# A Fourier neural operator on one core: the next image's beginning dealt out four pieces sooner, its statistics behind the row copies, ten head steps in a new order

## The chip, the cores and the metric

One core of a Trainium2 chip runs the whole program. The metric is device time in microseconds (us) for one execution of all eight images; lower is better. Five engines work side by side[...]: TensorE (PE in the profile, with its weight loads as PEld), VectorE (DVE), ScalarE (ACT), GpSimd (POOL) and SyncE (SP, which here only starts transfers).

## What is computed

For each of 8 images (8 channels of 256x256, four groups of two channels) the reference normalizes x by group, runs a Fourier neural operator and adds x; then it normalizes the sum by group, takes a 3x3 maximum around each pixel, and adds again.

```python
h = _gconv1x1(concat(x, grid), fc0_w, fc0_b)
for i in range(4):                       # the four "layers"
    h1 = _spectral_conv(h, sp_w1[i], sp_w2[i])   # rfft2, 24x12 modes kept and mixed, irfft2
    h2 = _gconv1x1(h, w_w[i], w_b[i])
    h = h1 + h2
    if i < 3:
        h = _gswish(h, betas[i])
h = _gswish(_gconv1x1(h, fc1_w, fc1_b), betas[3])   # 10 -> 128 per group
return _gconv1x1(h, fc2_w, fc2_b)                   # 128 -> 2 per group: "the head"
x = x + that;  x = x + dilate3x3(_gn(x))
```

## The kernel before, in words

Everything is float32. An image's state h lies in SBUF as 11 chunks of rows (`NCH`), each 128 partitions x 4 x 512. A layer has three parts. `mix` (line 403) multiplies the kept modes by the layer's weights on VectorE: twelve operations n = 0 to 11, products (L411) and sums (L414) in turn. `rows_even` (L474) or `rows_odd` (L496) turns the mixed spectrum into values for every row: TensorE writes p_g in PSUM, and VectorE (L217) and ScalarE (L215) copy it to the tile zt. `layer` (L534) then runs a `burst` per chunk (L580): TensorE adds the 1x1 convolution (L590, or L587 in layer 0) and the inverse transform along the row (L593, reads zt) into p_z, and ScalarE writes p_z back to h (L598, or L600 in layer 3). In layer 3 each chunk of h is then stored to DRAM.

Two further streams are woven into the layers.

- The head of the image before: 128 steps f (`first`, L803: TensorE L813, then ScalarE L814 and L815 into a tile act, of which there are 4) and 64 steps c (`second`, L818: TensorE L830 on two act tiles, then a VectorE addition L839, or L837 for the first of an output tile). The addition of a step c follows at once; that of a step C is only put into VectorE's queue at the next f (`sum_up`, L772).
- The next image's beginning, `start` (L673): `spectrum_x` (L265, statistics of x, its normalization and its small spectrum) and then `mix` for layer 0. It is a Python generator; each `yield` in it ends a piece, and whoever holds the generator takes a piece with `next`.

No scheduler decides the order: the block under `tc.manual_schedule` (L919) takes PE, DVE, ACT and SP instructions as the generators give them out. Each string that `layers` yields is a list of head steps to be put in at that place (`step`, L899); "t" takes a piece of the dilation of the image before that (`tail`).

In layer 3, the generator of the next image is taken from at 24 places: once after each of the two halves of `rows_odd` (L523), and twice per chunk in `layer`: after the steps "fct", and again after the "f" behind them (L612 and L615). Here "side piece" means such a piece, "first place" and "second place" mean those two. What is left of the generator after layer 3 is taken in `rest` (L680), one piece at a time, each followed by the steps of one entry of `REST` (L43); after each entry one chunk of the next image's x (two for image 0) is read into h (`read_x`, four transfers on SP).

PSUM has two rings: "one", two buffers of a bank, and "tri", two of three banks. A burst, a step f, the p_g of a half of the rows, and the fold p_f (L455) take one of each (`ps_four`); a step c and each TensorE piece of `spectrum_x` take a "one" (`ps_a`). A buffer comes free when the copy that reads it is done.

While image 0 runs there is no head, and only image 0's own pieces fill the queues; the code calls this `alone`.

Of the kernel before, what the change touches and what calls it, by code (L numbers as in the profile page):

```python
# [34 lines left out]
NCH = 11  # L35
# [4 lines left out]
DR = 2  # L40
STEPS = 128
BEHIND = mybir.DependencyInfo(mybir.DependencyClass.Sync, mybir.DependencyReason.DATA)
REST = ("ff", "f", "f", "fC", "fc"), ("f", "fc", "ffC", "ff", "fc")  # L43


@with_exitstack
def fno_dilate_kernel(ctx: ExitStack, tc: tile.TileContext, a: dict, out: bass.AP):
# [11 lines left out]
    def ps_a(name):  # L59
        return ps.tile([128, 512], F32, tag="one", bufs=2, name=name)  # L60
# [8 lines left out]
    def part(i):  # L69
        return slice(32 * i, 32 * i + 32)  # L70


    n_img = a["x"].shape[0]
# [191 lines left out]
    def spectrum_x(b, out_):  # L265

        x = turned[:, 0:2].rearrange("p i (g f) -> p i g f", g=G)
        st = sb.tile([128, G, 2, 6], F32, tag="bn", bufs=1, name=f"bn_x{b}")
        for i in range(2):
            for g in range(G):  # L270
                nc.vector.bn_stats(st[:, g, i, :], x[:, i, g])
            yield
        mv = sb.tile([128, G, 2], F32, tag="mvx", name=f"mv_x{b}")
        for g in range(G):
            nc.vector.bn_aggr(mv[:, g], st[:, g].rearrange("p n s -> p (n s)"))
        yield
        yield
        yield
        p = ps_a(f"p_st_x{b}")
        group_means(p, mv[:, :, 0])  # L280
        mr = sb.tile([128, 2, G + 1], F32, tag="mrx", name=f"mr_x{b}")
        d = sb.tile([128, 2, G + 1], F32, tag="dx", bufs=1, name=f"d_x{b}")
        nc.vector.tensor_copy(mr[:, 0], p[:, : G + 1])
        dm = d[:, 0, :G]
        nc.vector.tensor_tensor(dm, mv[:, :, 0], mr[:, 0, :G], ALU.subtract)
        nc.vector.tensor_tensor(dm, dm, dm, ALU.mult)
        nc.vector.tensor_tensor(dm, dm, mv[:, :, 1], ALU.add)
        yield
        yield
        q = ps_a(f"p_sv_x{b}")  # L290
        group_means(q, dm)
        nc.vector.tensor_scalar(d[:, 1], q[:, : G + 1], EPS, None, ALU.add)
        rsqrt(d[:, 1], mr[:, 1], d[:, 0])
        out_["mr"] = mr[:, :, G]
        for g in range(G):
            nc.vector.tensor_scalar(
                x[:, :, g], x[:, :, g], mr[:, 0, g : g + 1], mr[:, 1, g : g + 1], ALU.subtract, ALU.mult)
            if g != 1:
                yield
        yield  # L300

        a1, a2 = turned[:, 2, 0:512], turned[:, 2, 512:1024]
        a3 = turned[:, 2, 1024:1216].rearrange("p (g m) -> p g m", g=G)
        nc.vector.memset(a3, 0.0)
        p = ps_a(f"p_a1_{b}")
        for i in range(2):
            for g in range(G):
                mm(p[part(g)], er[:, i, :], x[:, i, g], start=i == 0, stop=i == 1)
        nc.vector.tensor_copy(a1, p)
        yield  # L310
        yield
        t = ps_a(f"p_a2_{b}")
        for i in range(4):
            nc.tensor.transpose(t[:, 128 * i : 128 * (i + 1)], a1[:, 128 * i : 128 * (i + 1)], ident)
        nc.vector.tensor_copy(a2, t)
        yield
        yield
        p = ps_a(f"p_a3_{b}")
        for j in range(2):
            for i in range(2):  # L320
                mm(p[:, 24 * j : 24 * j + 24], a2[:, 256 * j + 128 * i : 256 * j + 128 * i + 128], fw[:, i, 0:24],
                   start=i == 0, stop=i == 1)
        for g in range(G):
            nc.vector.tensor_copy(a3[part(g), g, :], p[part(g), 0:48])
        yield
        yield
        cols = a3.rearrange("p g (j k) -> p g j k", j=2)
        p = ps_a(f"p_xs_{b}")
        for k in range(2):
            for term in range(2):  # L330
                for q in range(4):
                    k0 = 12 * term + 3 * q
                    mm(p[part(q), 24 * k : 24 * k + 24], unf[:, spectrum_table(k, term), :],
                       cols[:, :, :, k0 : k0 + 3], start=term == 0, stop=term == 1)
        xe4 = xe.rearrange("p (s k) g j -> p s g j k", s=2)
        for k in range(2):
            nc.vector.tensor_copy(
                xe4[:, k, :, 0:2, :],
                p[:, 24 * k : 24 * k + 24].rearrange("p (g j k) -> p g j k", g=G, j=2),
            )  # L340
        yield
        bt = sb.tile([128, 2, 3, G, WID], F32, tag="B", bufs=1, name=f"B_{b}_0")
        prod = turned[:, 0, :1200].rearrange("p (i g o j) -> p i g o j", i=6, g=G, o=WID)
        for i in range(6):
            nc.vector.tensor_tensor(
                prod[:, i], wext, xe[:, i].unsqueeze(2).to_broadcast([128, G, WID, 5]), ALU.mult
            )
        nc.vector.tensor_reduce(
            bt.rearrange("p s k g o -> p (s k g o)"),
            prod.rearrange("p i g o j -> p (i g o) j"), AX.X, ALU.add,  # L350
        )
        out_["bt"] = bt
        yield
        yield

    def spectrum_table(k, term):

# [45 lines left out]
    def mix(b, l, out_):  # L403
# [3 lines left out]
        for n in range(12):  # L407
            k, k2 = n // 4, n // 2 % 2
            pr = turned[:, 2, 1024 * k2 : 1024 * k2 + 800].rearrange("p (g m i) -> p g m i", g=G, i=WID)
            if n % 2 == 0:  # L410
                nc.vector.tensor_tensor(  # L411
                    pr, sw[k], bt[:, k2, k].unsqueeze(2).to_broadcast([128, G, 2 * WID, WID]), ALU.mult)
            else:
                nc.vector.tensor_reduce(  # L414
                    s[k2][:, k].rearrange("p s o g -> p (s o) g"),
                    pr.rearrange("p g m i -> p m g i"), AX.X, ALU.add,
                )
            if l == 0:
                if n % 2 or n > 7:
                    yield  # L420
            elif n not in (0, 2, 6, 10):
                yield {1: "fc", 4: "fC", 7: "fC", 9: "fC"}.get(n, "f")
            if n == 2 and l == 3 and b + 1 < n_img:
                load_x(b + 1)
# [71 lines left out]
    def rows_odd(b, l, side):  # L496

        zv = zt[:, :, :, : NBLK * WID].rearrange("p r g (n o) -> p g o n r", n=NBLK)
        hold()
        yield "ffc"  # L500
        for part_of, by_act, kinds in ((((0, 1, 2), (3, 4, 5)), (2, 3), "fc"), (((9,), (6, 7, 8)), (1, 4, 5), "f")):
            one, tri, banks = ps_four(f"p_g_{b}_{l}_{part_of[0][0]}")
            pairs = []
            for i, os in enumerate(part_of):
                for at, o in enumerate(os):
                    for j in range(NQ):
                        for k in range(2):
                            two = slice(64 * k, 64 * k + 64)
                            last = mm(banks[2 * i + k][part(j), 2 * NBLK * CS * at : 2 * NBLK * CS * (at + 1)],
                                      fz2[two, o, :], rowg[two, j].rearrange("p g x -> p (g x)"),  # L510
                                      start=True, stop=True)
                for k in range(2):
                    src = banks[2 * i + k][:, : 2 * NBLK * CS * len(os)]
                    src = src.rearrange("p (o g n r) -> p g o n r", g=2, n=NBLK, r=CS)
                    dst = zv[:, 2 * k : 2 * k + 2, os[0] : os[-1] + 1]
                    if len(os) == 1:
                        pairs.append((dst[:, :, 0], src[:, :, 0]))
                    else:
                        pairs += [(dst[:, g], src[:, g]) for g in range(2)]
            copy_banks(pairs, by_act)  # L520
            yield kinds
            if l == 3:
                next(side, None)  # L523
        hold(last)
        if l < 3:
            yield "t"


    def read_x(b, c):
        if b < n_img:  # L530
            for g in range(G):
                nc.sync.dma_start(h[32 * g : 32 * g + 6, c].rearrange("p f w -> p (f w)"), a["xp"][b, c, g])
# [146 lines left out]

    def rest(b, then):  # L680
        c = 0 if b == 0 else NCH - 4
        for n, _ in enumerate(then):
            yield REST[b > 0][n]
            for _ in range(2 if b == 0 else 1):
                if c < NCH:
                    read_x(b + 1, c)
                    c += 1
        for i in range(c, NCH):
            read_x(b + 1, i)

    def layers(b, stored, d, then, ahead):

# [431 lines left out]
```

## Time and profile before

| what | value |
|---|---|
| median of 3 runs (lowest to highest) | 3705.54 us (3701.52 to 3706.05) |
| the profiled execution: time, and the span of its instructions | 3705.41 us, 3703.6 us |
| PE, DVE, ACT busy (share of the span) | 3495.7 us (94%), 2385.4 us (64%), 2864.6 us (77%) |
| mean granted TensorE clock | 0.977 |
| layer 3's rows of images 1, 2, 5, 6, from the first p_g to the first L593 of burst 0 | 9.9 us each; 10.8 us in images 3 and 4 |
| the last burst of layer 3 (first L593) to the fold p_f of the next image | 20.0 us in images 1, 2, 4, 5; 21.7 us in images 3 and 6 |

The page's first section gives each engine's busy time; its fourth the chain of work that ended last, by engine and line; its fifth the groups of equal instructions, with the idle time of the engine just before them and what ended it. A line of the timeline gives start, duration, engine, source line, operation, "out<-in", shapes, and in brackets the idle time ahead and who ended it. A line of the waits gives who waited for whom, the total in us, how often, and the longest.

### The profile page before, as it was taken

What the parts mean: (1) busy time and instruction counts of PE and PEld (TensorE: products, weight loads), DVE (VectorE), ACT (ScalarE), POOL (GpSimd) and SP (SyncE); (2) the same over time, 40 slices, a digit from 0 to 9 for tenths busy, and PEclk for the clock granted to TensorE, in tenths of its full rate; (3) what the DMA queues carried; (4) which work ended last, traced back from release to release, by engine and by line L of the source; (5) the groups of instructions that cost most, each with busy time, mean ns of one, the idle gap of its engine ahead of it and who ended that gap; (6) DMA issues with size and microseconds to landing.
All of it is one profiled execution on the core that took longest, in us unless ns stands there. A gap on an engine that the chain in (4) does not pass through costs nothing.

```text
span 3703.6 us, 112658 instructions
## 1 busy us (share of the span) xinstructions
PE 3495.7 (94%) x50872; PEld 1271.0 (34%) x50872; DVE 2385.4 (64%) x3711; ACT 2864.6 (77%) x3021; POOL 117.1 (3%) x202
## 2 busy tenths in 40 slices
PE   5768999999999999999999999999999999999997
PEld 2323333333333333333333333333333333333222
DVE  6776666557775677746776577765777567772443
ACT  2435888888788888787887878888888878879986
POOL 1000000000000000000000000000000000000000
PEclk7878999999999999999999999999999999999998
DMA  3005111432225212261223512244222522225221
GB/s 91 16 19 205 52 50 46 160 110 72 72 83 190 81 55 66 92 220 52 60 62 125 181 55 74 65 159 122 64 75 89 183 76 61 72 64 194 82 83 48
DMA packets 114081, 344.71 MB, mean 93 GB/s; under 512 B 15985, under 2 KB 18481, under 8 KB 98177
## 3 DMA queue, kind: packets, MB, share of 16 engines
q1 hardware_dynamic: 95392, 276.32, 24.6%
q0 software_dynamic: 18208, 61.18, 5.0%
q8 instruction: 400, 6.55, 0.7%
q14 instruction: 81, 0.66, 0.1%
HBM read 213.44 MB, written 123.74 MB: 91 GB/s over the span
## 4 chain that ended last, share of the span: by engine, by line
PE 73%; DVE 16%; issue 4%; ACT 4%; DMA 2%; POOL 0%; ACTq 0%; DVEq 0%; POOLq 0%
PE p_fc L830 20%; PE p_fc L813 19%; PE p_z L593 9%; PE p_z L590 7%; PE p_d L558 7%; PE p_z L587 3%; DVE y L839 3%; PE p_u L572 3%; DVE turned L541 3%; DVE S L414 3%; DVE turned L411 2%; DMA yin<-y_rows 2%; PE p_b L381 1%; ACT act L815 1%; ACT act L814 1%
## 5 line engine op out<-in xcount | busy, mean ns | idle before, releaser
L815 ACT ACTIVATE act<-p_fc 128x1536 f32<-128x1536 f32 x1024 | 1493.1, 1458 | 0.0
L813 PE MATMUL p_fc<-hs,c_w 32*128 32x512 f32 x8192 | 1133.2, 625 | 40.2 <-DVE y L839 20.8
L830 PE MATMUL p_fc<-act,c_w 128*32 128x512 f32 x8192 | 1008.6, 601 | 0.2 <-ACT act L815 0.2
L814 ACT ACTIVATE act<-p_fc 128x512 f32<-128x512 f32 x1024 | 616.5, 602 | 229.7 <-PE p_fc L813 218.2
L541 DVE STREAM_TRANSPOSE turned<-h 128x1024 f32<-128x1024 f32 x528 | 632.7, 1226 | 189.7 <-ACT h L598 189.2
L598 ACT ACTIVATE h<-p_z 128x512 f32<-128x512 f32 (+1 forms) x528 | 511.9, 1021 | 212.2 <-PE p_z L593 212.2
L839 DVE TENSOR_TENSOR y<-p_fc,y 128x512 f32<-128x512 f32 x392 | 267.7, 683 | 553.9 <-PE p_fc L830 553.9
L813 PEld LDWEIGHTS p_fc<-hs,c_w 32*128 32x128 f32 x8192 | 357.7, 183 | 612.8 <-ACT act L814 253.3
L830 PEld LDWEIGHTS p_fc<-act,c_w 128*32 128x32 f32 x8192 | 221.8, 109 | 705.0 <-issue 330.7
L593 PE MATMUL p_z<-c_binv,zt 32*128 32x256 f32 x5632 | 411.7, 406 | 2.1 <-DVE zt L217 2.1
L590 PE MATMUL p_z<-h,c_wt 32*32 32x512 f32 x8448 | 363.5, 606 | 15.7 <-DVE zt L217 7.7
L593 PEld LDWEIGHTS p_z<-c_binv,zt 32*128 32x128 f32 x5632 | 259.8, 187 | 312.4 <-issue 300.0
L558 PE MATMUL p_d<-turned,c_fw 32*32 32x480 f32 (+1 forms) x9216 | 307.8, 539 | 0.6 <-DVE turned L541 0.2
L600 ACT ACTIVATE h<-p_z,c_bias 128x512 f32<-128x512 f32 (+1 forms) x176 | 186.4, 1110 | 89.1 <-PE p_z L593 89.0
L562 ACT ACTIVATE turned<-p_d 128x1440 f32<-128x1440 f32 x144 | 182.9, 1270 | 89.7 <-PE p_d L558 86.5
L215 ACT ACTIVATE zt<-p_g 128x198 f32<-128x198 f32 (+2 forms) x118 | 53.4, 575 | 182.8 <-PE p_g L487 99.9
L414 DVE TENSOR_REDUCE S<-turned 128x80 f32<-128x800 f32 x192 | 189.0, 984 | 5.9
L411 DVE TENSOR_TENSOR turned<-t,B 128x800 f32<-128x800 f32 x192 | 188.7, 983 | 0.9
L558 PEld LDWEIGHTS p_d<-turned,c_fw 32*32 32x32 f32 x9216 | 127.0, 103 | 165.8 <-issue 64.9
L372 DVE STREAM_TRANSPOSE turned<-zt 128x960 f32<-128x960 f32 x96 | 176.8, 1865 | 2.5
L590 PEld LDWEIGHTS p_z<-h,c_wt 32*32 32x32 f32 x8448 | 93.2, 103 | 186.8 <-DVE y L839 48.8
L572 PE MATMUL p_u<-turned,c_stack 128*32 128x480 f32 (+1 forms) x1152 | 136.7, 543 | 11.6 <-DVE turned L561 6.2
(192 smaller groups left out, 1762.8 us busy)
## 6 DMA issues: line engine op xcount, KB each, us to landing
stored<-h SPq DMA_DIRECT2D x88, 1024.0 KB
hs<-stored SPq DMA_DIRECT2D x352, 256.0 KB
t<-in_spw SPq DMA_DIRECT2D x96, 400.0 KB
yin<-y_rows POOLq DMA_DIRECT2D x56, 512.0 KB, 5.2
h<-in_xp SPq DMA_DIRECT2D x352, 48.0 KB
turned<-in_xw SPq DMA_DIRECT2D x16, 1024.0 KB
y<-in_x SPq DMA_DIRECT2D x56, 256.0 KB
y_rows<-y POOLq DMA_DIRECT2D x56, 256.0 KB, 3.9
```

Source lines behind the costliest of these rows:

```text
L411: nc.vector.tensor_tensor(pr, sw[k], bt[:, k2, k].unsqueeze(2).to_broadcast([128, G, 2 * WID, WID]), ALU.mult)
L414: nc.vector.tensor_reduce(s[k2][:, k].rearrange("p s o g -> p (s o) g"), pr.rearrange("p g m i -> p m g i"), AX.X, ALU.add,)
L541: nc.vector.transpose(dst[:, 2 * i : 2 * i + 2], h[:, c, 2 * i : 2 * i + 2].rearrange("p f (s x) -> p f s x", s=2))
L558: mm(banks[q][part(v % 4), : 240 * n], fw8[part(q), v, :], t[part(q), :, :, v, : NBLK * WID], start=v < 4, stop=v >= 4)
L590: mm(o, wt[part(q), l, g, :], h[part(q), c, f, :], start=True, stop=False)
L593: mm(banks[q][:, HW * s : HW * (s + 1)], zt[part(q), 2 * c + s].rearrange("p f o -> p (f o)"), binv[part(q), :], start=False, stop=s == 1)
L598: nc.scalar.activation(dst, src, AF.Silu)
L813: mm(banks[g], w1[part(g), blk, :], hs[k][part(g), :], start=True, stop=True)
L814: nc.scalar.activation(act[:, 0, :], one, AF.Silu)
L815: nc.scalar.activation(act[:, 1:4, :], tri, AF.Silu)
L830: mm(acc[part(g), :], w2[:, g, 15 - rb - i : 47 - rb - i], act[:, g, :], start=i == 0, stop=i == 1)
L839: nc.vector.tensor_tensor(y, sums, y, ALU.add)
```

## The change

Three things move; no arithmetic is added or taken away.

1. In `rows_odd` of layer 3 both pieces of the next image are taken behind the second half's copies and steps, no longer one behind each half. These pieces are the statistics of x: twice four bn_stats (L271).
2. Four yields are deleted: one behind the aggregation in `spectrum_x`, one behind its end, and two in layer 0's `mix` (n = 8 and n = 10). Later pieces so come one place sooner, then two, then four. All twelve operations of `mix` now lie in layer 3, where operations 8 to 11 stood in `rest`.
3. `rest` takes the two pieces left (the sums L432 and L433, then the fold) behind an entry of ten head steps in all, split in two; the reads of x follow an entry in lots of up to six chunks. Written as one row, the steps were "f fc ffC ff fc" and are "ffc ffCffcf"; for image 0 they were "ff f f fC fc" and are "fff ffCfc".

```diff
-REST = ("ff", "f", "f", "fC", "fc"), ("f", "fc", "ffC", "ff", "fc")
+REST = ("fff", "ffCfc"), ("ffc", "ffCffcf")
...
             nc.vector.bn_aggr(mv[:, g], st[:, g].rearrange("p n s -> p (n s)"))
         yield
         yield
-        yield
         p = ps_a(f"p_st_x{b}")
...
         out_["bt"] = bt
-        yield
         yield
...
             if l == 0:
-                if n % 2 or n > 7:
+                if n % 2:
                     yield
...
             copy_banks(pairs, by_act)
             yield kinds
-            if l == 3:
-                next(side, None)
+        for _ in range(2 if l == 3 else 0):
+            next(side, None)
         hold(last)
...
         c = 0 if b == 0 else NCH - 4
-        for n, _ in enumerate(then):
+        if b + 1 == n_img:
+            return
+        for n in range(2):
             yield REST[b > 0][n]
-            for _ in range(2 if b == 0 else 1):
-                if c < NCH:
-                    read_x(b + 1, c)
-                    c += 1
-        for i in range(c, NCH):
-            read_x(b + 1, i)
+            for i in range(c + 6 * n, min(c + 6 * n + 6, NCH)):
+                read_x(b + 1, i)
+            next(then, None)
```

## The prediction

> **What bounds the kernel now.** I read the page first: TensorE is busy 94% of the span, no other engine over 77%, and the chain that ended last runs 73% on TensorE. So what counts is where TensorE stands still.
>
> ```profile
> PE 3495.7 (94%) x50872; PEld 1271.0 (34%) x50872; DVE 2385.4 (64%) x3711; ACT 2864.6 (77%) x3021; POOL 117.1 (3%) x202
> PE 73%; DVE 16%; issue 4%; ACT 4%; DMA 2%; POOL 0%; ACTq 0%; DVEq 0%; POOLq 0%
> ```
>
> The waits of TensorE have two rows at the edited places (columns: us in total, times, longest).
>
> ```profile
> PE p_fc L813 <- DVE y L839: 20.8, 41, 1.8
> PE p_z L590 <- DVE zt L217: 7.7, 6, 1.3
> ```
>
> The second comes once in each of images 1 to 6, in layer 3's rows; image 2's timeline shows it:
>
> ```profile
> 1128.28 1.20 PE L509 MATMUL p_g<-c_rowg,fz 64*32 64x132 f32 x64
> 1129.03 2.46 DVE L271 BATCH_NORM_STATS2 bn_x<-turned 128x6 f32<-128x512 f32 x4
> 1129.52 1.09 ACT L215 ACTIVATE zt<-p_g 128x132 f32<-128x132 f32 x3 [1.01 <-PE p_g L509]
> 1131.40 1.06 DVE L217 COPY zt<-p_g 128x132 f32<-128x132 f32 x3
> 1131.83 1.92 PE L590 MATMUL p_z<-h,c_wt 32*32 32x512 f32 x32 [1.27 <-DVE zt L217]
> 1133.69 1.15 PE L593 MATMUL p_z<-c_binv,zt 32*128 32x256 f32 x16
> ```
>
> p_g is ready at 1129.48, but VectorE is at x's statistics until 1131.49; burst 0 needs that PSUM back. The other stall is behind layer 3, where `mix` stands ahead of a head addition:
>
> ```profile
> 1209.75 0.99 DVE L414 TENSOR_REDUCE S<-turned 128x80 f32<-128x800 f32 x1
> 1210.65 0.68 DVE L839 TENSOR_TENSOR y<-p_fc,y 128x512 f32<-128x512 f32 x1
> 1211.39 1.14 PE L813 MATMUL p_fc<-hs,c_w 32*128 32x512 f32 x8 [1.81 <-DVE y L839]
> ```
>
> [...] just behind these stalls the clock column (the last but two) falls to half for 3.4 us at 1571.5 and 2015.3 (rows, images 3 and 4), 1653.5 and 2974.4 (behind layer 3, images 3 and 6).
>
> ```profile
> 1562.70:1571.50 8.80, 7.52 (x198) 3.48 (x194) 7.14 (x16) 7.09 (x10) 0.00 (x0) 1.00 0.18 50
> 1571.50:1574.90 3.40, 3.40 (x43) 1.53 (x46) 2.19 (x4) 0.01 (x1) 0.00 (x0) 0.50 0.12 34
> ```
>
> [...] both waits shown above are for PSUM.
>
> **The change part by part**, per image, against the profiled 3705.4 us (span 3703.6; the median of the runs, 3705.5, is the same within 0.1).
>
> *Rows: −1.97 us in each of images 1 to 6.* With the eight bn_stats behind the copies, VectorE's three copies run 1129.5 to 1130.55 (1.06), ScalarE's end at 1130.61 as before. The head step ends near 1130.5, so burst 0 starts there and its large part at 1130.67; L590 to L593 takes 1.07 elsewhere (1186.80 to 1187.88). L593 at 1131.7 instead of 1133.69. Cover: the eight (4.9 us) end at 1135.5, just as the next head addition falls due (step c ends 1135.5); were they later, burst 1 would wait for it. Image 0 has no head; there L593 waits for zt itself (2.10 us, at 300.22) and could start at 298.1; its chain of side pieces moves along: −2.0.
>
> *Four pieces sooner: +2.40 us in images 2 to 6, +0.47 in image 1.* This is the hidden cost. The built order shows each TensorE side piece going from the second place (behind f) to the first (between c and f). Its "one" buffer shifts the ring: the f behind it now waits for the addition of the c just ahead, and the burst for the side piece's copy (or, for p_a L314 and L321 of images 2 to 6, for that f's ScalarE pass). From image 2:
>
> ```profile
> 1171.28 1.14 PE L813 MATMUL p_fc<-hs,c_w 32*128 32x512 f32 x8
> 1171.38 0.69 DVE L839 TENSOR_TENSOR y<-p_fc,y 128x512 f32<-128x512 f32 x1 [4.18 <-PE p_fc L830]
> 1172.35 0.66 PE L314 MATMUL p_a<-ident,turned 128*128 128x128 f32 x4
> 1173.10 0.24 PEld L590 LDWEIGHTS p_z<-h,c_wt 32*32 32x32 f32 x32 [0.34 <-ACT act L814]
> ```
>
> Let E be the end of c (1171.28). The addition lets f go at E+0.86 (1171.38 + 0.69 + 0.05 to start), or behind the side piece if that is longer. Then burst is 1.82 later where it waits for f's ScalarE pass (1171.28 to 1173.10), else 1.08, or when the copy is done. E to burst, before and after: p_st 1.83, 2.38 (0.86 + 1.08 would be 1.94; but its copy L283 stands behind a dilation piece and ends at 2.33); p_sv 1.83, 1.94; p_a L308 2.93, 2.95; p_a L314 1.82, 2.68; p_a L321 2.07, 2.82 (piece of 1.0, then 1.82); p_xs 1.83, 1.94. Sum of losses 0.55 + 0.11 + 0.02 + 0.86 + 0.75 + 0.11 = 2.40. Image 1 has no dilation beside it and waits for copies alone: 0.47. The four L411/L414 now in chunk 10 cost nothing: chunks 8 to 10 get 4 x 0.97 + 0.69 (+ 0.69) us of VectorE in 6.24 us. Uncovered, they would hold up the next burst by what exceeds that.
>
> *Behind layer 3: −1.8 us in each of images 1 to 6.* The new row of steps hardly differs: written out, only the last f and c change places, and for image 0 the order is the same as before, so it gains nothing. What counts is that `mix` is gone from VectorE: its last sum ends near 1208.8, the addition of the c at 1206.58 at 1209.45, so f goes at 1209.5, not 1211.39. From there TensorE's f 1.07 and c 1.87 follow each other without a wait over 0.1: p_f at 1217.5 instead of 1220.38. Then some comes back: f stands ahead of p_f, so the f behind waits for its ScalarE pass (until 1219.6), and p_g starts at 1223.6 instead of 1225.37: 1.8. The four chunk reads (16 transfers) are queued on SP ahead of the hs load of a later f; it is asked for three chunks early, and SP is through by about 1212 (before: 1217.3 for that load), so I cost it at 0. For image 0 24 reads go ahead of one hs load; that lands near 356, due at about 370: 0. POOL's order is unchanged, and the early return for image 7 skips a loop that was empty.
>
> *Half-clock windows: −6.5 us.* Against the undisturbed images the four windows cost 1.57 (10.78 − 9.91 and 6.94 − 6.24), 1.62, 1.65 and 1.64 us. With their stalls gone, I let them go. The unknown is whether the new waits (0.55 to 0.86 us each, 15 in all) set off others. Old stalls did in 4 of 12; these are under half as long: between 0 and 4, I take 1: +1.6.
>
> Sum: rows −11.8 − 2.0, side pieces +12.5, behind layer 3 −10.8, windows −6.5 + 1.6: −17.0, so 3688.4; I say 3688.
>
> **The rivals.** (a) *Nothing left over.* The ScalarE passes bound the stretch behind layer 3 (13.74 of 16.2 us busy in the window 1204.18 to 1220.38), its 1.8 and its windows stay; then −13.8 + 12.5 − 3.2 = −4.5: 3701. For it: seven f are some 14 us of ScalarE. Against: my walk starts its passes earlier, from 1209.6. (b) *The ring costs nothing*, because the side pieces' copies and additions finish sooner than I put them: −17 − 12.5: 3676. Against: the 0.86 is read from rows. (c) *Slower: the clock.* If the new waits set off half-clock windows at 18 of the 36 moved side pieces, that is 18 x 1.65 = 29.7 against the 18.6 of gains: 3716.5. It decides from 12 windows on. [...] against: L590 waiting 1.3 us did it only twice in six. That the change does not do what it says is excluded by the built order, apart from image 0's steps.
>
> **How the numbers follow.** Likeliest 0.72: 3688, own range 3682 to 3697. (a) 0.17, (b) 0.05, (c) 0.06. The low end takes no new window and lets the three others in the trace go too (301.8, 1677.3, 3547.8: about 5 us more): 3682, with 2 us for run to run 3680. The high end takes in (a): 3701. 0.2% is 7.4 us, about what a measurement can tell from no change. Faster: 0.70 + 0.05 + 0.03 of (a) = 0.78; same 0.16; slower 0.06.
>
> **What would show it.** Right: L217 of the rows' second half starts with p_g's end, and rows to L593 fall from 9.9 to 7.9 us; the row "p_fc L813 <- DVE y L839" of 1.8 goes; last burst to p_f from 20.0 to about 17; burst to burst longer by 0.5 to 0.9 in three places of images 2 to 6. Wrong: those three unchanged, or half-clock windows inside layer 3.

## The result and the profile after

The changed kernel takes 3692.22 us (median of 10 runs, 3687.88 to 3697.89) against 3704.36 us (3699.55 to 3706.50, 10 runs) of the kernel before, measured beside it: a ratio of 0.997, 95% interval 0.996 to 0.998, some 12 us less. The profiled execution took 3691.78 us with a span of 3690.0 (before: 3705.41 and 3703.6). Lines have moved by two or three: L507, L588, L591 are the old L509, L590, L593, and L810, L827, L836 the old L813, L830, L839.

The page's busy times and its chain of work, by engine:

```profile
PE 3488.5 (95%) x50872; PEld 1272.9 (34%) x50872; DVE 2385.6 (65%) x3711; ACT 2871.0 (78%) x3021; POOL 117.0 (3%) x202
PE 76%; DVE 16%; issue 4%; DMA 2%; ACT 2%; POOL 0%; ACTq 0%; DVEq 0%; POOLq 0%; SPq 0%
```

TensorE still bounds the kernel; ScalarE's share of the chain fell from 4% to 2%. Four rows of what TensorE waited for (us in total, times, longest):

```profile
PE p_fc L810 <- DVE y L836: 17.5, 59, 0.5
PE p_z L588 <- ACT act L811: 7.3, 10, 0.7
PE p_g L485 <- DVE zt L217: 2.6, 6, 0.4
PE p_z L588 <- DVE mr_x L282: 1.9, 5, 0.4
```

The old row of p_z waiting for zt (7.7 us, 6 times) is gone. So are the six stalls of 1.8 in the row of p_fc and y, but this row now has 59 waits instead of 41 and still 17.5 us. Two of the rows shown are new: waits of p_g for L217, and of p_z for mr_x. The row for act was 4.2 us before (18 times, 0.3 at most).

The rows of layer 3 in image 2, on the timeline:

```profile
1123.37 1.20 PE L507 MATMUL p_g<-c_rowg,fz 64*32 64x132 f32 x64
1124.12 1.36 DVE L217 COPY zt<-p_g 128x132 f32<-128x132 f32 x3
1125.33 4.80 DVE L271 BATCH_NORM_STATS2 bn_x<-turned 128x6 f32<-128x512 f32 x8
1125.58 1.35 PE L588 MATMUL p_z<-h,c_wt 32*32 32x512 f32 x32
1126.86 1.15 PE L591 MATMUL p_z<-c_binv,zt 32*128 32x256 f32 x16
1130.79 0.69 DVE L836 TENSOR_TENSOR y<-p_fc,y 128x512 f32<-128x512 f32 x1 [0.66 <-PE p_fc L827]
```

The copies follow p_g at once and L588 starts without a wait. The eight bn_stats end at 1130.13, and VectorE then still idles 0.66 us until the next addition's input is there: the cover held.

Behind layer 3 of the same image, at the place of the old 1.81 us stall, the last sum of `mix` ends at 1204.68 and the addition follows. The two steps f (16 matmuls) follow c without a wait:

```profile
1202.45 1.93 PE L827 MATMUL p_fc<-act,c_w 128*32 128x512 f32 x16
1203.69 0.99 DVE L412 TENSOR_REDUCE S<-turned 128x80 f32<-128x800 f32 x1
1204.30 2.17 PE L810 MATMUL p_fc<-hs,c_w 32*128 32x512 f32 x16
1204.60 0.68 DVE L836 TENSOR_TENSOR y<-p_fc,y 128x512 f32<-128x512 f32 x1
```

### The profile page after: what moved, and what is told of

It is laid out like the page before. It is cut to its first block, busy times and chain, and to the rows that moved or that the text cites. A ratio compares the mean times of both kernels' runs of the same rounds, so it can differ in the third digit from the quotient of the medians.

```text
span 3690.0 us, 112652 instructions
## 1 busy us (share of the span) xinstructions
PE 3488.5 (95%) x50872; PEld 1272.9 (34%) x50872; DVE 2385.6 (65%) x3711; ACT 2871.0 (78%) x3021; POOL 117.0 (3%) x202
## 4 chain that ended last, share of the span: by engine, by line
PE 76%; DVE 16%; issue 4%; DMA 2%; ACT 2%; POOL 0%; ACTq 0%; DVEq 0%; POOLq 0%; SPq 0%
PE p_fc L827 21%; PE p_fc L810 21%; PE p_z L591 9%; PE p_d L556 7%; PE p_z L588 7%; PE p_z L585 3%; DVE y L836 3%; PE p_u L570 3%; DVE turned L539 3%; DVE S L412 2%; DVE turned L409 2%; DMA yin<-y_rows 2%; DVE turned L370 1%; PE p_g L507 1%; PE p_b L379 1%
## 5 line engine op out<-in xcount | busy, mean ns | idle before, releaser
L810 PE MATMUL p_fc<-hs,c_w 32*128 32x512 f32 x8192 | 1134.9, 626 | 36.8 <-DVE y L836 17.5
L827 PE MATMUL p_fc<-act,c_w 128*32 128x512 f32 x8192 | 1007.9, 599 | 0.2 <-ACT act L812 0.2
L836 DVE TENSOR_TENSOR y<-p_fc,y 128x512 f32<-128x512 f32 x392 | 267.9, 683 | 543.6 <-PE p_fc L827 543.6
L810 PEld LDWEIGHTS p_fc<-hs,c_w 32*128 32x128 f32 x8192 | 359.3, 183 | 585.4 <-ACT act L811 227.0
L827 PEld LDWEIGHTS p_fc<-act,c_w 128*32 128x32 f32 x8192 | 222.5, 109 | 705.0 <-issue 332.6
L591 PE MATMUL p_z<-c_binv,zt 32*128 32x256 f32 x5632 | 411.0, 406 | 0.0
L588 PE MATMUL p_z<-h,c_wt 32*32 32x512 f32 x8448 | 356.8, 602 | 12.3 <-ACT act L811 7.3
L591 PEld LDWEIGHTS p_z<-c_binv,zt 32*128 32x128 f32 x5632 | 259.0, 187 | 307.6 <-issue 294.4
L588 PEld LDWEIGHTS p_z<-h,c_wt 32*32 32x32 f32 x8448 | 93.8, 103 | 198.1 <-DVE y L836 48.8
```

What stands on the lines that cost most here:

```text
L588: mm(o, wt[part(q), l, g, :], h[part(q), c, f, :], start=True, stop=False)
L591: mm(banks[q][:, HW * s : HW * (s + 1)], zt[part(q), 2 * c + s].rearrange("p f o -> p (f o)"), binv[part(q), :], start=False, stop=s == 1)
L810: mm(banks[g], w1[part(g), blk, :], hs[k][part(g), :], start=True, stop=True)
L827: mm(acc[part(g), :], w2[:, g, 15 - rb - i : 47 - rb - i], act[:, g, :], start=i == 0, stop=i == 1)
L836: nc.vector.tensor_tensor(y, sums, y, ALU.add)
```

## The experiments

All times are medians, each beside runs of the kernel before on the same chip. "Layer 3" in this table is the stretch in the trace from the first row product p_g to the next image's first burst in layer 0, in us; half-clock windows that lie in it stand in brackets. (Image 0's stretch begins at half clock, for 2.7 us before and 2.8 us after; in no row is that counted.)

| kernel | image 0 | image 1 | images 2 to 6, each |
|---|---|---|---|
| before | 64.9 (one window) | 108.05 | 108.05 (images 3, 4, 6: 111.3, 109.7, 109.7; two windows, one, one) |
| after | 62.6 | 105.6 | 107.1 |
| rows alone | 62.9 | 106.2 | 106.2 (images 2, 6: 107.8; one window each) |
| first places alone | 63.4 | 110.9 (one window) | 110.75 (image 2: 112.45; one window) |
| second places | 67.9 (three windows) | 104.4 | 104.4 |
| by image | 63.1; again 64.4 | 104.45 | 104.45 |
| early mix alone | 65.0 (one window) | 106.4 | 106.4 |
| without the rows | 65.9 (one window) | 107.5 | 109.0 (image 3: 110.7; one window) |

**The rows alone.** Kernel before with one edit:

```diff
-            if l == 3:
-                next(side, None)
+        for _ in range(2 if l == 3 else 0):
+            next(side, None)
```

> The kernel before with the first part alone: both pieces of statistics behind the second half's copies. Theory (the sum of the prediction, its terms as measured in the changed kernel's trace): rows -1.92 us in images 1 to 6, image 0 -2.3, nothing else moves, and the half-clock windows in the rows of images 3 and 4 go (some -3): -14 to -17, so 3688 to 3691 us beside 3704.4, and burst to burst and last burst to p_f as before (6.73 and 20.0 us). Rival (the gain comes from the steps behind layer 3 alone): 3702 to 3705 us.

Measured: 3689.99 us (3687.34 to 3691.65) against 3705.89; ratio 0.9956 (0.9944 to 0.9968). As the theory has it: this third of the change is worth at least as much as the whole. Not all of the 15.9 us is the rows' own: the trace has four half-clock windows where that of before has seven. It keeps the other stall, shown by the row of its waits and by the timeline of image 2:

```profile
PE p_fc L813 <- DVE y L839: 20.8, 41, 1.8
```

```profile
1204.72 0.99 DVE L414 TENSOR_REDUCE S<-turned 128x80 f32<-128x800 f32 x1
1205.63 0.68 DVE L839 TENSOR_TENSOR y<-p_fc,y 128x512 f32<-128x512 f32 x1
1206.36 1.14 PE L813 MATMUL p_fc<-hs,c_w 32*128 32x512 f32 x8 [1.80 <-DVE y L839]
```

**The first places alone.** Kernel before with one yield moved, so that only the pieces from p_st to the end of `spectrum_x` come one place sooner:

```diff
         yield
         yield
-        yield
         p = ps_a(f"p_st_x{b}")
...
         out_["bt"] = bt
+        yield
         yield
         yield
```

> The kernel before with one yield moved from behind the aggregation to behind the small spectrum's end: the TensorE side pieces alone go from the second place (behind f) to the first (between c and f), the number of pieces and all else stay. Theory (the ring's waits cost what the trace of the changed kernel shows): 5 x 2.71 + 1.17 = +14.7 us, so about 3719 us, with burst to burst longer by 0.56, 0.13, 0.03, 1.05, 0.81 and 0.13 us. Rival (the ring costs nothing by itself, its waits only take over idle time made elsewhere): 3704 us, within 2 us.

Measured: 3717.19 us (3714.48 to 3723.61); ratio 1.0033 (1.0021 to 1.0045): 11 to 12 us slower than the kernel before beside it. The ring's cost is real. Its waits:

```profile
PE p_fc L813 <- DVE y L839: 28.3, 65, 1.8
PE p_z L590 <- ACT act L814: 7.3, 10, 0.7
```

The second row is the changed kernel's to the digit, so it belongs to the moved pieces. The first can be taken apart: six stalls of 1.8 (10.8 us), 35 waits of 10.0 us in all, which kernels without both costs still have, and 24 waits of 7.5 us that came with the pieces. The layer 3 spacings of images 1 to 6 give +14.7 us, as in the changed kernel. The difference to 11.3 is mostly half-clock windows, of which this trace has four and that of before seven: image 0 is 1.5 us shorter because the window in it is gone, and layer 3 of the other images has two windows (3.4 us) where before has four (6.5).

**Second places.** The changed kernel with the pieces of `spectrum_x` a chunk earlier than before, at the second place instead of the first:

```diff
                 nc.vector.bn_stats(st[:, g, i, :], x[:, i, g])
-            yield
+            if i == 0:
+                yield
...
         out_["bt"] = bt
+        yield
         yield
```

> The changed kernel with one more yield deleted (between the second statistics and the aggregation) and one put back behind the small spectrum: the TensorE side pieces lie one chunk earlier, at the second place again (behind f), and the mix still ends in layer 3. Theory (the first place is what costs): the 14.7 us of the ring come back, nothing else changes: 3692.2 - 14.7 = 3677.5 us, up to 3681 if the earlier aggregation delays a head addition. Rival (four pieces sooner cost by their VectorE work, wherever they lie): 3691 to 3694 us.

Measured: 3682.09 us (3680.38 to 3685.55) against 3705.89; ratio 0.9937 (0.9925 to 0.9949). That is some 24 us less than before, where the changed kernel gained 12. The theory's direction holds. In layer 3 of images 1 to 6 it holds fully: the burst spacings are again those of the kernel before, one chunk earlier, 1.1 us less than the changed kernel in image 1 and 2.7 in each of the five others, 14.5 in all. The same piece (p_a, L313 and L314) in image 2, first in the changed kernel, then here:

```profile
1163.43 1.92 PE L827 MATMUL p_fc<-act,c_w 128*32 128x512 f32 x16
1165.28 0.66 PE L313 MATMUL p_a<-ident,turned 128*128 128x128 f32 x4
1165.42 0.69 DVE L836 TENSOR_TENSOR y<-p_fc,y 128x512 f32<-128x512 f32 x1 [5.38 <-PE p_fc L827]
1166.16 1.14 PE L810 MATMUL p_fc<-hs,c_w 32*128 32x512 f32 x8 [0.23 <-DVE y L836]
1168.03 1.15 PE L588 MATMUL p_z<-h,c_wt 32*32 32x512 f32 x32 [0.73 <-ACT act L811]
```

```profile
1160.83 1.92 PE L829 MATMUL p_fc<-act,c_w 128*32 128x512 f32 x16
1162.71 1.14 PE L812 MATMUL p_fc<-hs,c_w 32*128 32x512 f32 x8
1163.79 0.66 PE L314 MATMUL p_a<-ident,turned 128*128 128x128 f32 x4
1164.54 1.15 PE L590 MATMUL p_z<-h,c_wt 32*32 32x512 f32 x32
```

Between c and f (above), the piece takes the "one" buffer that f would have had: f waits for the addition of the c just ahead and starts 0.88 us behind the end of c, and the burst waits for f's ScalarE pass, 2.75 us behind it. Behind f (below), nothing waits, and the burst starts after 1.83 us.

Some 3 us of the 14.5 did not show in the median. Image 0's layer 3 is 5.3 us longer than in the changed kernel: with no head to fill the time, p_st stands 3.7 instead of 1.5 us for the statistics, and three half-clock windows follow.

```profile
PE p_st_x L260 <- DVE mv_x L276: 3.7, 1, 3.7
```

**By image.** The kernel above, with image 1's beginning (which runs in image 0's layer 3) back at the changed kernel's places:

```diff
-            if i == 0:
+            if i == 0 or b < 2:
                 yield
...
-        yield
+        if b > 1:
+            yield
         yield
```

> This is e4_second_places with image 0 put back to the changed kernel's places: the side pieces of images 2 to 6's beginnings stand a chunk earlier at the second place, those of image 1's beginning (taken while image 0 runs, with no head beside them) where the changed kernel has them. Theory: e4_second_places got back all of the ring's cost (its layer 3 of images 1 to 6 is shorter by 1.1 and five times 2.7 us, 14.5 in all) and lost 5.3 us in image 0, where p_st waits 3.7 instead of 1.5 us for the statistics and three half-clock windows follow. So 3682.1 - 5.3 = 3676.8, between 3674 and 3679; in the trace the wait of p_st for mv_x in image 0 is 1.5 us again and image 0's layer 3 takes 62.6 us. Rival: image 0 is not where the rest was lost, and what e4_second_places left is new half-clock windows: then about 3682, as there.

Measured: 3681.28 us (3675.97 to 3684.87), ratio 0.9928 (0.9914 to 0.9942). A miss for the size. Image 0 did get its 4.8 us back (63.1, and p_st waits 1.5), but the median is only as good as that of the kernel above. Its trace, of the slowest of its six runs (3684.87), has half-clock windows just behind five of the seven starts of layer 0 from image 1 on, where the changed kernel has them behind three and the one above behind one. One of them, in windows of the profile (busy times by engine, then TensorE's granted clock, DMA share, GB/s):

```profile
1663.79:1667.20 3.41, 3.41 (x83) 1.37 (x80) 0.20 (x2) 2.88 (x6) 0.00 (x0) 1.00 0.02 5
1667.20:1670.62 3.42, 3.42 (x39) 1.93 (x24) 2.10 (x2) 1.91 (x3) 0.00 (x0) 0.50 0.00 0
```

**Without the rows, and the early mix alone.** Two kernels that share one edit, statistics between the halves of the rows again, made once on the changed kernel and once on "by image":

```diff
-        for _ in range(2 if l == 3 else 0):
-            next(side, None)
+            if l == 3:
+                next(side, None)
```

> This is the changed kernel with x's statistics back between the halves of the rows: four pieces sooner and the new steps behind layer 3, without the rows' part. Theory: the three parts add up. The rows alone were worth 15.9 us (e1_rows_only), so 3692.2 + 15.9 = 3708, between 3704 and 3711: the side pieces cost 14.7 and the stretch behind layer 3 gives back 10.4 and two half-clock windows. Rival: the parts do not add up, because the statistics' later place lengthens the stretch in which the pieces sooner are felt; then about 3696 to 3700, nearer the changed kernel.

Measured: 3703.78 us (3700.36 to 3709.38) against 3707.23, ratio 0.9992 (0.9982 to 1.0001): pieces sooner and early mix together are worth little or nothing. It lies just under the theory's 3704 and above the rival's 3696 to 3700. Beside its own runs of the kernel before it is 3.4 us faster, though, where the theory's parts (+14.7, -10.4 and two windows) meant about 1 us slower. With the 15.9 of the rows alone the medians so add up to 19.3 us, for the 12.1 of the whole; that gap is no wider than the three intervals together. In layer 3 the parts do add up (the burst spacings and the stretch behind layer 3 are the changed kernel's to 0.02 us, the rows those of before); its trace has two half-clock windows where that of before has seven, and the mean granted clock of its runs was 0.978 to 0.980, that of the runs of before beside it 0.973 to 0.979.

> This is e6_by_image with x's statistics back between the halves of layer 3's rows: the early mix and the new steps behind layer 3 alone, with the ring's cost taken out. Theory: the stretch behind layer 3 is worth its 1.7 us in each of images 1 to 6 without the rows' part, and two half-clock windows there go: 3705.9 - 10.4 - 3.3 = 3692, between 3689 and 3696; the wait of L812 for the addition L838 of 1.8 us is gone, that of L590 for the rows' copy L217 (1.3 us, 6 times) is back. Rival: the ScalarE passes bound that stretch and only the earlier rows made room: then 3702 or more, with the fold no sooner than 20.0 us after the last burst.

Measured: 3692.74 us (3690.64 to 3695.70), ratio 0.9964 (0.9951 to 0.9976). As the theory has it: 14.5 us less than before beside it, for a forecast of 13.7. Layer 3 is 1.7 us shorter in each of images 1 to 6 with the rows as before, so the stretch behind it needs no help from them. Its waits:

```profile
PE p_fc L813 <- DVE y L839: 10.0, 35, 0.4
PE p_z L591 <- DVE zt L217: 7.7, 6, 1.3
```

The six stalls of 1.8 are gone and no new ones have come: these are the 35 waits left when both mix and the ring's cost are out.

**The old order of the steps.** The changed kernel with its ten steps in the order that they had before:

```diff
-REST = ("fff", "ffCfc"), ("ffc", "ffCffcf")
+REST = ("fff", "ffCfc"), ("ffc", "ffCfffc")
```

> The changed kernel with the ten head steps behind layer 3 in their former order (the second entry ends f f f c in place of f f c f). Theory (the gain behind layer 3 comes from the mix having left VectorE, not from the order): within 2 us of the changed kernel, 3692 us; last burst to p_f longer by some 1 us, p_f to p_g shorter by as much. Rival (the order is the gain): the 1.73 us in images 1 to 6 are lost, 3702.6 us.

Measured: 3691.61 us (3689.95 to 3694.24), ratio 0.9961 (0.9949 to 0.9973), the changed kernel's time. Image 2 behind layer 3, in the changed kernel and here:

```profile
1213.65 0.88 PE L453 MATMUL p_f<-fs,c_fold 32*32 32x72 f32 x64
1219.50 0.73 PE L485 MATMUL p_g<-c_rowg,fz 32*128 32x264 f32 x8
```

```profile
1214.01 0.88 PE L453 MATMUL p_f<-fs,c_fold 32*32 32x72 f32 x64
1218.99 0.73 PE L485 MATMUL p_g<-c_rowg,fz 32*128 32x264 f32 x8
```

The new order brings the fold p_f 0.86 us forward (17.43 instead of 18.29 behind the last burst) and hands it back before p_g (5.86 instead of 4.99). The gain is mix's leaving alone.

**What is left: the half-clock windows.** Two more kernels: "by image" once more, unchanged, and "by image" with a head step between layer 0's first two bursts.

```diff
-                yield "t"
+                yield "t" if l else "tf"
                 burst(1)
-                yield "f"
+                yield "f" if l else ""
```

> This is e6_by_image with one step f of layer 0 put between that layer's first two bursts instead of behind them. In the traces so far the granted clock changes only at the borders of a grid of 3.41 us, and 15 of 63 starts of layer 0 are followed by a half-clock window: all where the first burst begins 2.94 to 3.41 us or up to 0.17 us into a grid cell, so that its two bursts of six-row matmuls lie in one cell, and none elsewhere. Theory: [...] With eight full matmuls of an f between the two bursts no window follows layer 0's start at any place in the cell: 3673 to 3678, if the new order adds no wait. Rival: the windows follow something else at that place (the p_g rows, or the earlier light work): they stay, about one in four starts, and the time is e6_by_image's, 3679 to 3683.

Measured: 3682.47 us (3680.12 to 3687.72), ratio 0.9943 (0.9931 to 0.9956). No window in any image from 1 on, and yet no gain: its images from 1 on follow each other at 436.2 to 437.6 us from rows to rows, those of the two traces of "by image" without a window at 435.4 to 436.4. The new order itself so seems to cost about 1 us an image; where is open. On the cause of the windows it tells nothing: none of its seven starts of layer 0 fell into the part of the grid that its expectation names.

> This is e6_by_image unchanged, a second time, beside the kernel above. Theory: its layer 3 is the same to 0.1 us in every image and only the half-clock windows behind layer 0's start come in other images or in other numbers; with one or two of the usual seven instead of five, 3675 to 3679. Rival (the missing 4 us are a lasting cost of its order): again 3681, with five such windows at the same places.

Measured: 3680.08 us (3676.84 to 3682.66), ratio 0.9931 (0.9917 to 0.9945), between the two. Layer 3 of images 1 to 6 is the same to 0.02 us and the windows came in other images (two behind layer 0's start instead of five). Image 0 took 64.4 us this time, 0.7 us of it TensorE waiting for nothing that the profile shows. So two executions of one kernel had their windows at different places. Against their own runs of the kernel before, the two measurements of "by image" gain 26.0 and 24.0 us and "second places" 23.8, and each has an interval of some 4 to 5 us to either side: whether part of the 5 us that image 0 gave back is really lost cannot be told from these runs.

## Why the prediction was nearly right, and what in it was off

The direction held, and so did the mechanisms in images 1 to 6; that for image 0 did not. The time came out 4 us above the forecast, inside its range. By its own terms, trace against trace (predicted -17.0, measured -13.6; the medians differ by 12.1):

- *Rows, -11.8 and -2.0.* Measured 7.99 instead of 9.91, -1.92 in each of six images: -11.5. L591 follows as worked out, and the cover named (the eight bn_stats before the next addition) held with 0.66 us to spare. The rows alone, run by themselves, confirm it. In image 0 the stretch is 2.3 us shorter (62.6 for 64.9), near the -2.0, but by luck. Its L591 does come 2.1 us sooner, yet the side pieces do not move along: the eight bn_stats (4.79 us) and the aggregation now end at 303.15, and TensorE's p_st stands waiting for them (the wait in image 0):

```profile
PE p_st_x L260 <- DVE mv_x L275: 1.5, 1, 1.5
```

"First places alone", which has the old rows there but no half-clock window where that of before stands (301.8), takes 63.4 us. So the rows gave some 0.8 us, and about 1.5 is that window's going.

- *Four pieces sooner, +12.5.* This term was too small: +14.7. The chain "f waits for the addition, the burst for f's ScalarE pass" came as worked out (0.88 and 2.75 us behind c's end, predicted 0.86 and 2.68). What the working left out is the f behind the burst. In image 2 the f ahead has its second ScalarE pass until 1162.32; the f behind the burst starts at 1162.31, three of its matmuls are held until that pass is over, and all eight take 1.19 us instead of 1.04. With this p_a L314 cost 1.05, not 0.86. Image 1, costed at 0.47 as if only copies counted, pays 1.17: there the f behind the burst takes 1.18 or 1.19 at all six pieces, and the f ahead waits for its addition (0.23 to 0.53 us) at four. The rival that the ring costs nothing fell with "first places alone".
- *Mix in chunk 10 at nothing.* Held: the last two spacings are 6.24 us as before.
- *Behind layer 3, -10.8.* Measured -2.59 to p_f and +0.86 from p_f to p_g, -1.73 a time: -10.4. The rival that ScalarE leaves nothing over fell with "early mix alone". That the order does nothing is shown by the kernel with the old one. No wait of TensorE's names an hs load, so nothing shows that the reads on SP cost anything, as said.
- *Half-clock windows, -6.5 and +1.6.* The four at the old stalls went, 6.5 us of layer 3, and none came at the new waits, the longest of which is 0.73 us: the rival for slower did not come about. But windows came where the sum didn't look: behind three starts of layer 0 where before had one (+3.3). Of the three others, which only the low end of the forecast let go, that at 3547.8 went with 1.7 us and that in image 0 with the 1.5 above. Without the latter the net is -4.9, the number predicted, by luck: none of the 1.6 came where it was put.

Together, -11.5 and -0.8 for the rows, +14.7, -10.4 and -6.4 for the windows make -14.4. Image 0's rows start 0.4 us later in the trace of after, and layers 0 to 2, which differ by some tenths from image to image, have the other 0.4 to the -13.6 measured. So without windows the three parts are worth 8.0 us. The rest of the gain in these two traces is nearly all windows, and these came at different places in the two traces of "by image".

## What to carry to other kernels

Putting an operation that takes a buffer from a shared ring one place sooner changes who gets which buffer: count the ring, and find for each instruction behind it whose release it now waits for. Here this took back more than half of what the other two parts gained in layer 3 and behind it; one place further, a whole chunk sooner at the old position, it cost nothing in images 1 to 6, but image 0, which has no head, became 5.3 us longer. A part of a change that frees a queue (mix off VectorE, statistics behind the copies) should be run by itself before the places of everything else are moved with it.

## What the runs showed of the hardware

The clock here is TensorE's granted clock as the profile records it. Between 295.5 and 3667 us it fell to 0.50 for 3.41 us at a time, seven times in the trace of before and three times in that of after. In each of the two traces, all changes of this record lie within 0.001 us of one grid with a spacing of 3.41 us; its cells are meant below. Of the twelve stalls of before in layer 3's rows (1.3 us) and behind layer 3 (1.8 us), seven lie wholly in one cell. Four of the seven were followed by a cell at half clock, which by the prediction's comparison with undisturbed images cost 1.57 to 1.65 us on top; of the five that cross a border, none was. What sets the four apart from the other three is open.

A half-clock cell also came with TensorE shown busy for all 3.41 us of the cell ahead. In the changed kernel (windows cut at the grid; the third number from the end is the clock), and the timeline of the same place:

```profile
1664.15:1667.56 3.41, 3.41 (x83) 1.31 (x80) 0.05 (x1) 2.88 (x5) 0.00 (x0) 1.00 0.02 5
1667.56:1670.97 3.41, 3.41 (x40) 1.92 (x24) 2.24 (x2) 2.04 (x3) 0.00 (x0) 0.50 0.00 0
```

```profile
1664.10 1.57 PE L585 MATMUL p_z<-h,wcn 6*32 6x512 f32 x32
1665.61 1.15 PE L591 MATMUL p_z<-c_binv,zt 32*128 32x256 f32 x16
1666.68 1.36 PE L585 MATMUL p_z<-h,wcn 6*32 6x512 f32 x32
1667.97 2.09 PE L591 MATMUL p_z<-c_binv,zt 32*128 32x256 f32 x16
```

The last line's 16 matmuls take 2.09 us instead of 1.15. Of the 14 starts of layer 0 in images 1 to 7 of before and after, the half-clock cell came behind four: those whose first burst began 2.95, 3.09 or 3.37 us into a cell (after) or 0.06 us into one (before). The other ten began 0.83 to 2.56 us into a cell. That the six rows of these bursts' matmuls are the cause was not shown.
